# Two borders of a convolution kernel: six products for the statistics, other PSUM banks, and two relus in another place

## The chip, the cores and the metric

The kernel runs on one core of one Trainium2 chip. The metric is the device time of one execution in microseconds (us). The engines are named as the profile names them: PE is TensorE, DVE is VectorE, ACT is ScalarE, POOL is GpSimd, and SP is SyncE, which here only issues DMAs.

## The reference

Two bottleneck blocks run one after the other on an input of 64 images, 1024 channels and 14x14 pixels, all in f32. Each block is

```
out = relu(bn(conv1x1(x,   1024 -> 256)))
out = relu(bn(conv3x3(out,  256 -> 256)))
out =      bn(conv1x1(out,  256 -> 1024))
x   = relu(x + softplus(residual_scale) * out)
```

and bn takes its mean and variance over all images and pixels of the batch (12,544 values a channel). So a norm's scale and shift are known only after the whole batch has been through the convolution in front of it.

## The kernel before, in words

There are 128 partitions (P), so 1024 channels are 8 slots of 128 (CS) and 256 channels are 2 (MS). The batch is cut into 32 tiles of two images (T tiles of PX = 392 pixels). The 256-channel activations y of the whole batch stay in on-chip memory; x is streamed from memory, tile by tile, and block 0 leaves its output in memory as mid.

A block has these stages. The first 1x1 convolution (for block 0 at the start; for block 1 it is fused with the end of block 0), the 3x3 convolution (`conv2`, whose loads, columns and sums fill most of the profile), the Gram stage with the statistics of the third convolution, and the third convolution with the residual.

The statistics of the third convolution are not taken from its output. Its output is linear in y, so the mean of an output channel is its weights times the mean of y, and its variance is the weights on both sides of the 256x256 Gram matrix of y. `gram` builds the Gram matrix on PE: it transposes pieces of y and multiplies them with themselves into two PSUM banks, `upper` and `lower`, of which only some 64-wide blocks are computed, each off-diagonal block once. `conv3_stats` (from L1178 on) then does the following:

- `scaled` (L1185) moves the blocks from PSUM into two 128x258 tiles g0 and g1 (one for each half of the channels) with a DVE multiply by 1/n, or 2/n for a block that stands for itself and its mirror image. The blocks that are not there are zeros.
- ACT copies one column (L1193), DVE makes by_mean, the weights times the means, in two rows of 128x1024 (L1201, L1202).
- For each half h of the output channels, PE makes two 128x512 products t0 and t1, one for each half of the columns of g, each summed over g0 and g1: four matmuls a half, eight in all. DVE multiplies them by the weights (L1213) and adds the two (L1214).
- Sixteen matmuls with ones sum over the partitions: eight of by_mean into bank ax, eight of the products into bank ap. From the two, `affine` makes scale and shift of each output channel in a chain of short DVE operations (L1338 to L1357, L1498), with a square root on ACT between.

The order of each engine comes from a scheduler, but matmuls, most ACT operations and some DVE operations are kept in program order (`keep_in_program_order`). PE's matmuls all go through the helper at L171, ACT's through the one at L334, so these two lines stand for many operations and the tile names tell them apart.

[...] In block 0 they are named cy (two), ay (two), cx, cp, ap and ax; in block 1 cy, cx and cp (two each), ap and ax. Whoever asks for a tag whose banks are taken waits until the last reader is done. `psum.cycle` gives the tags where no tag is asked for.

The third convolution of the first tile of a block (o runs over the 8 slots of output channels, one `conv3` each) is plain. The result for o = 0 is made before the statistics, to fill PE; then o = 1, and in block 1 also o = 2 to 5, are made after them, before the affine. The list of these is `made`. `residual` (L1225 on) then takes for each o the made tile, or makes it, adds it to x on DVE (L1233: x = result*scale + x), applies the relu with the shift on ACT (L1234), and after the last o stores the tile (L1239, on POOL's queue when a whole tile is stored).

After it the other tiles of block 0 go through `fused`: a seven-product scheme (class `Seven`, two slots of output channels and two halves of the pixels at a time) for the third convolution (class `Conv3`, banks with prefix c) which is interleaved matmul by matmul with the same scheme for the first convolution of block 1 (class `Conv1`, prefix a). The third convolution has a lead of LAG = 14 steps, so PE does those alone first:

```
        for i in range(LAG):
            next(c)
```

The first steps of such a stream are p1 (bank cy), p2 (bank cx), p6 (again into cy), p5 (bank cp) and p7 (cy again). Between p1 and p6, and between p6 and p7, ACT has to copy the sum so far out of cy (tile cu12, L334), so each waits for ACT. POOL adds these copies to x (L488, L493), ACT applies the relu, and ACT's queue stores the tile. In block 1, `final` runs the same scheme for pairs of tiles and stores the output from SP's queue, which also loads x from mid.

Of the kernel before, what the change touches and what calls it, by code (L numbers as in the profile page):

```python
# [41 lines left out]
P = 128  # L42
# [46 lines left out]
def bottlenecks(ctx: ExitStack, tc: tile.TileContext, x, w1s, w2s, w3s, pars, out):  # L89
# [79 lines left out]
    def matmul(*args, **kw):  # L169

        tc.keep_in_program_order(nc.tensor.matmul(*args, **kw))  # L171
# [1006 lines left out]
    def conv3_stats(psum, one, grams, w3, mv, tags, spare):  # L1178
# [7 lines left out]

        scaled(g0[low], 0, upper[low], by[0][low])
        scaled(g0[high], Q + 1, upper[high], by[0][high])
        scaled(g1[low], 2 * Q + 1, lower[low, : 2 * Q + 1], by[1][low])
        n = Q + 1  # L1190
        for a, k in (1, 0), (3 * Q + 1, 1):
            scaled(g1[high], a, lower[high, k * n : k * n + n], by[1][high, k * n : k * n + n])
# [12 lines left out]
        for h in range(2):  # L1205
            cols = slice(h * half, (h + 1) * half)
            t0, t1 = (psum.tile(half * P, tag) for tag in tags[2 * h : 2 * h + 2])
            for i, g in enumerate((g0, g1)):
                for n, t in enumerate((t0, t1)):
                    matmul(t, g[:, 1 + n * P : 1 + n * P + P], w3[:, i, cols, :], start=i == 0, stop=i == 1)  # L1210
            qs = [q[:, s, h * half * P : (h + 1) * half * P] for s in range(MS)]
            for s, t in ((0, t0), (1, t1)):
                nc.vector.tensor_mul(qs[s], t, w3[:, s, cols, :].rearrange("p o c -> p (o c)"))  # L1213
            nc.vector.tensor_add(qs[0], qs[0], qs[1])  # L1214
# [10 lines left out]
    def residual(psum, xt, b, t, w3, aff, made=()):  # L1225
# [4 lines left out]
        for o in range(CS):  # L1230
# [3 lines left out]
            nc.scalar.activation(v, v, AF.Relu, bias=shift[:, o : o + 1])  # L1234

            step = CS if not tail else 1 if o + 2 >= CS else 2
            if (o + 1) % step == 0:
                queue = nc.gpsimd if step == CS else nc.scalar if o + 1 == CS else nc.sync
                queue.dma_start(  # L1239
                    out=to[:, (o + 1 - step) * PX : (o + 1) * PX],  # L1240
                    in_=xt[:, o + 1 - step : o + 1, :].rearrange("p s f -> p (s f)"),
                )

# [26 lines left out]
    def fused(psum, pool, xpool, xs, w1, w3, aff, par, stats, one_done):  # L1270
# [185 lines left out]
    for b in range(2):  # L1456
# [7 lines left out]
        with tc.tile_pool(name=f"last_{b}", bufs=1) as one, tc.tile_pool(  # L1464
# [6 lines left out]
            with ExitStack() as scope:  # L1471
# [22 lines left out]
                if b == 1:  # L1494
                    made += [conv3(psum, 0, o, w3, tag) for o, tag in zip(range(2, 6), ("cy", "cp") * 2)]
# [4 lines left out]
                residual(psum, xs[0], b, 0, w3, aff, made)  # L1500
                weights = made_a + made_c
                with tc.tile_pool(name=f"rest_{b}", bufs=1) as pool:
# [5 lines left out]
                    fused(psum, pool, xpool, xs, *weights, aff, par[b + 1], stats1, one_done)  # L1508
# [40 lines left out]
```

## Time and profile before

| | us |
|---|---|
| median of 3 runs (lowest to highest) | 1932.78 (1932.09 to 1934.12) |
| time of the profiled execution | 1934.62 |
| its span in the profile | 1932.8 |
| busy in the span: PE, DVE, ACT, POOL | 1907.8, 1545.2, 1080.9, 563.8 |
| statistics of block 0 (first product with g to last sum) | 653.21 to about 663.6 |
| statistics of block 1 | 1614.98 to about 1625.4 |

A line of the timeline has the start in us, the duration in us, the engine, the line of kernel.py, the operation, the tile that is written and those that are read, the shapes, and how many records are taken together; in brackets follow the idle time of the engine just before it and what ended that. An f32 matmul of this kernel leaves two records. Matmuls overlap in the pipeline, so the distance from one start to the next tells what one costs. A line of the waits says who waited for whom, for how many us in total, how often, and the longest.

### The profile page before, as it was taken

What the parts mean: (1) busy time and instruction counts of PE and PEld (TensorE: products, weight loads), DVE (VectorE), ACT (ScalarE), POOL (GpSimd) and SP (SyncE); (2) the same over time, 40 slices, a digit from 0 to 9 for tenths busy, and PEclk for the clock granted to TensorE, in tenths of its full rate; (3) what the DMA queues carried; (4) which work ended last, traced back from release to release, by engine and by line L of the source; (5) the groups of instructions that cost most, each with busy time, mean ns of one, the idle gap of its engine ahead of it and who ended that gap; (6) DMA issues with size and microseconds to landing.
All of it is one profiled execution on the core that took longest, in us unless ns stands there. A gap on an engine that the chain in (4) does not pass through costs nothing.

```text
span 1932.8 us, 28746 instructions
## 1 busy us (share of the span) xinstructions
PE 1907.8 (99%) x10246; PEld 1602.5 (83%) x10246; DVE 1545.2 (80%) x2481; ACT 1080.9 (56%) x2142; POOL 563.8 (29%) x680
## 2 busy tenths in 40 slices
PE   9999999999999999999999999999999999999999
PEld 5555557999997799999999999989999977555555
DVE  5778767999997767676776767689999986888886
ACT  2222214677777255555555555556777682666666
POOL 0111100211204133333433334302121041666664
PEclk9999999999999999999999999999999999999999
DMA  7777634787946534444444444258788466899998
GB/s 290 276 244 271 229 136 156 198 221 208 226 153 178 183 150 184 168 167 171 180 183 167 167 174 179 115 179 211 215 206 225 131 175 228 289 326 337 338 339 302
DMA packets 199071, 409.56 MB, mean 212 GB/s; under 512 B 37168, under 2 KB 175536, under 8 KB 182416
## 3 DMA queue, kind: packets, MB, share of 16 engines
q1 hardware_dynamic: 160128, 322.40, 48.4%
q0 software_dynamic: 33184, 34.25, 8.6%
q10 hardware_dynamic: 5616, 51.06, 6.3%
q8 instruction: 81, 1.33, 0.3%
q14 instruction: 62, 0.51, 0.1%
HBM read 263.75 MB, written 115.34 MB: 196 GB/s over the span
## 4 chain that ended last, share of the span: by engine, by line
PE 93%; DVE 3%; DMA 1%; ACT 1%; issue 1%; SPq 0%; POOL 0%; DVEq 0%; ACTq 0%; POOLq 0%
PE cy L171 17%; PE ay L171 17%; PE columns L171 13%; PE cp L171 12%; PE ap L171 10%; PE m L171 7%; PE l L171 6%; PE cx L171 5%; PE ax L171 4%; PE ps L171 1%; ACT y L334 0%; DMA home<-y 0%; DMA x<-mid 0%; SPq L1065 0%; DMA ws<-y 0%
## 5 line engine op out<-in xcount | busy, mean ns | idle before, releaser
L334 ACT ACTIVATE cu<-cy,scale 128x196 f32<-128x196 f32 (+1 forms) x552 | 256.8, 474 | 276.9 <-PE cy L171 271.7
L171 PE MATMUL columns<-v,ub 128*128 128x224 f32 (+1 forms) x1536 | 300.7, 337 | 0.0
L334 ACT ACTIVATE x<-x,shift 128x392 f32<-128x392 f32 x428 | 241.0, 613 | 59.6 <-POOL x L493 53.1
L171 PEld LDWEIGHTS columns<-v,ub 128*128 128x128 f32 x1536 | 269.2, 188 | 2.8
L467 DVE SCALAR_TENSOR_TENSOR x<-cp,scale,x 128x196 f32<-128x196 f32 (+1 forms) x368 | 178.0, 484 | 97.8 <-PE cp L171 96.5
L171 PE MATMUL cy<-ct,ws 128*128 128x196 f32 (+1 forms) x736 | 221.9, 383 | 1.8 <-ACT cu L334 1.7
L488 POOL TENSOR_TENSOR x<-x,cu 128x196 f32<-128x196 f32 (+1 forms) x184 | 159.7, 868 | 172.9 <-ACT cu L334 165.0
L171 PE MATMUL ay<-at,ws 128*128 128x196 f32 (+1 forms) x752 | 209.1, 381 | 0.0
L493 POOL TENSOR_TENSOR x<-x,cu 128x392 f32<-128x392 f32 x124 | 125.8, 1014 | 191.5 <-DVE x L467 191.5
L171 PEld LDWEIGHTS ay<-at,ws 128*128 128x128 f32 x752 | 136.5, 190 | 33.4
L171 PEld LDWEIGHTS cy<-ct,ws 128*128 128x128 f32 x736 | 133.4, 190 | 37.0 <-ACT cu L334 5.3
L171 PE MATMUL l<-diffs,ub 128*128 128x224 f32 (+1 forms) x768 | 149.1, 337 | 2.6 <-PE columns L171 2.6
L514 POOL TENSOR_TENSOR x<-x,cu 128x392 f32<-128x392 f32 x120 | 122.0, 1017 | 86.2 <-DVE x L467 71.8
L171 PE MATMUL m<-sums,ua 128*128 128x224 f32 (+1 forms) x752 | 145.9, 337 | 1.1 <-DVE sums L625 1.1
L334 ACT ACTIVATE au<-ay 128x196 f32<-128x196 f32 (+1 forms) x141 | 53.8, 381 | 156.9 <-PE ay L171 152.1
L171 PEld LDWEIGHTS l<-diffs,ub 128*128 128x128 f32 x768 | 134.3, 189 | 4.4 <-PE columns L171 3.9
L467 DVE SCALAR_TENSOR_TENSOR x<-cx,scale,x 128x196 f32<-128x196 f32 (+1 forms) x184 | 89.0, 484 | 57.0 <-PE cx L171 56.8
L171 PEld LDWEIGHTS m<-sums,ua 128*128 128x128 f32 x752 | 131.3, 189 | 2.9 <-DVE sums L625 2.5
L171 PE MATMUL cy<-y,w 128*128 128x196 f32 (+1 forms) x408 | 125.3, 393 | 0.0
L171 PE MATMUL cx<-y,w 128*128 128x196 f32 (+1 forms) x400 | 122.7, 391 | 0.0
L171 PE MATMUL cp<-y,ws 128*128 128x196 f32 (+1 forms) x368 | 113.6, 390 | 0.2 <-DVE x L467 0.2
L761 ACT ACTIVATE columns<-m 128x448 f32<-128x448 f32 (+1 forms) x160 | 78.5, 490 | 59.4 <-PE m L171 56.8
(219 smaller groups left out, 3973.1 us busy)
## 6 DMA issues: line engine op xcount, KB each, us to landing
x<-in_x SPq DMA_DIRECT2D x62, 1568.0 KB, 6.6
ub<-u SPq DMA_DIRECT2D x94, 768.0 KB, 5.3
x<-mid SPq DMA_DIRECT2D x32, 1568.0 KB, 7.8
mid<-x ACTq DMA_DIRECT2D x31, 1568.0 KB, 5.1
out<-x SPq DMA_DIRECT2D x123, 392.0 KB, 5.4
ua<-u SPq DMA_DIRECT2D x94, 256.0 KB, 3.0
u<-y POOLq DMA_DIRECT2D x48, 256.0 KB, 5.6
home<-y SPq DMA_DIRECT2D x72, 96.0 KB, 3.6
```

The lines of the kernel that those rows point to most:

```text
L171: tc.keep_in_program_order(nc.tensor.matmul(*args, **kw))
L334: tc.keep_in_program_order(nc.scalar.activation(*args, **kw))
L467: nc.vector.scalar_tensor_tensor(v, bank, self.scale[:, o : o + 1], v, ALU.mult, ALU.add)
L488: nc.gpsimd.tensor_add(self.part(1, 1), self.part(1, 1), u3)
L493: nc.gpsimd.tensor_add(v, v, self.u12)
L514: nc.gpsimd.tensor_add(v, v, self.u12[:, i * self.n : (i + 1) * self.n])
L761: nc.scalar.activation(v, m, AF.Copy)
```

## The change

There are three edits, of which the first concerns both blocks and the others only block 0.

1. In `conv3_stats` the block of the Gram matrix that stood left of the diagonal (rows of g1, columns of g0's half) is transposed on PE into bank ax and copied by DVE into the empty place of g0 that mirrors it. With it the left half of g1 holds nothing that a product needs, so t0 takes one matmul (g0) and t1 two (g0 and g1): six in all instead of eight. The block to be transposed is scaled first in the source.
2. In block 0, `made` holds five tiles before the affine instead of two, with tags ay, ay, cy, cx, cy, and the tags of the last three are given by a new `psum.cycle`.
3. In block 0, the relus of the last two output slots of the first tile and its store are not issued in `residual`. They are collected in a list, and `fused` issues them after the third step of the stream's lead. The relus now go through the helper at L334.

```diff
@@ conv3_stats
+        n = Q + 1
+        scaled(g1[high], 1, lower[high, :n], by[1][high, :n])
+        turned = psum.tile(P, "ax")
+        tc.keep_in_program_order(nc.tensor.transpose(turned, g1[:, 1 : P + 1], ident))
         scaled(g0[low], 0, upper[low], by[0][low])
         scaled(g0[high], Q + 1, upper[high], by[0][high])
+        nc.vector.tensor_copy(g0[low, 3 * Q + 1 : M + 1], turned[low, Q:])
         scaled(g1[low], 2 * Q + 1, lower[low, : 2 * Q + 1], by[1][low])
-        n = Q + 1
-        for a, k in (1, 0), (3 * Q + 1, 1):
-            scaled(g1[high], a, lower[high, k * n : k * n + n], by[1][high, k * n : k * n + n])
+        scaled(g1[high], 3 * Q + 1, lower[high, n : 2 * n], by[1][high, n : 2 * n])
...
-            for i, g in enumerate((g0, g1)):
-                for n, t in enumerate((t0, t1)):
-                    matmul(t, g[:, 1 + n * P : 1 + n * P + P], w3[:, i, cols, :], start=i == 0, stop=i == 1)
+            left, right = slice(1, P + 1), slice(P + 1, M + 1)
+            matmul(t0, g0[:, left], w3[:, 0, cols, :], start=True, stop=True)
+            matmul(t1, g0[:, right], w3[:, 0, cols, :], start=True, stop=False)
+            matmul(t1, g1[:, right], w3[:, 1, cols, :], start=False, stop=True)
@@ residual
-            nc.scalar.activation(v, v, AF.Relu, bias=shift[:, o : o + 1])
+            relu = partial(act, v, v, AF.Relu, bias=shift[:, o : o + 1])
+            if later is not None and o + 2 >= CS:
+                later.append(relu)
+            else:
+                relu()
...
-                queue.dma_start(
+                store = partial(
+                    queue.dma_start,
...
+                if later is not None:
+                    later.append(store)
+                else:
+                    store()
@@ fused
         for i in range(LAG):
             next(c)
+            if i == 2:
+                for run in begun:
+                    run()
@@ bottlenecks
-                if b == 1:
-                    made += [conv3(psum, 0, o, w3, tag) for o, tag in zip(range(2, 6), ("cy", "cp") * 2)]
+                tags = ("cy", "cp") * 2 if b else ("cy", "cx", "cy")
+                made += [conv3(psum, 0, 2 + i, w3, tag) for i, tag in enumerate(tags)]
+                if b == 0:
+                    psum.cycle = itertools.cycle(["ay", "ay", "cy"])
...
-                residual(psum, xs[0], b, 0, w3, aff, made)
+                later = None if b else []
+                residual(psum, xs[0], b, 0, w3, aff, made, later)
...
-                    fused(psum, pool, xpool, xs, *weights, aff, par[b + 1], stats1, one_done)
+                    fused(psum, pool, xpool, xs, *weights, aff, par[b + 1], stats1, one_done, later)
```

More of the change, by code (lines that the diff above doesn't have):

```diff
@@ L1223, in conv3_stats, with residual @@
         nc.vector.tensor_sub(mv[:, :, 1], mv[:, :, 1], sq)
-    def residual(psum, xt, b, t, w3, aff, made=()):
+    def residual(psum, xt, b, t, w3, aff, made=(), later=None):
         scale, shift = aff
@@ L1268, in final, with fused @@
         residual(psum, xs[T - 1], 1, T - 1, a, aff)
-    def fused(psum, pool, xpool, xs, w1, w3, aff, par, stats, one_done):
+    def fused(psum, pool, xpool, xs, w1, w3, aff, par, stats, one_done, begun):
         def last_convs():
```

## The prediction

> **What bounds the kernel now.** I read the page's busy line first, then the chain of work that ended last, then PE's own waits between 653 and 690 us, and then the timeline of PE and DVE at the two borders (about 651 to 690 us for block 0, 1613 to 1640 us for block 1).
>
> ```profile
> PE 1907.8 (99%) x10246; PEld 1602.5 (83%) x10246; DVE 1545.2 (80%) x2481; ACT 1080.9 (56%) x2142; POOL 563.8 (29%) x680
> PE 93%; DVE 3%; DMA 1%; ACT 1%; issue 1%; SPq 0%; POOL 0%; DVEq 0%; ACTq 0%; POOLq 0%
> ```
>
> PE is busy 99% of the span and makes 93% of the chain. So a microsecond counts if it is PE work, or PE's waiting, and only there. The waits of PE in the first border:
>
> ```profile
> PE cy L171 <- ACT cu L334: 1.6, 3, 1.0
> PE ay L171 <- DVE x L1233: 1.2, 1, 1.2
> ```
>
> The timeline of PE shows where they stand:
>
> ```profile
> 653.21 1.02 PE L171 MATMUL cy<-w,g 128*128 128x512 f32 x2
> 654.07 1.02 PE L171 MATMUL cp<-w,g 128*128 128x512 f32 x2
> ...
> 660.08 1.89 PE L171 MATMUL ax<-ones,home 128*128 128x64 f32 x16
> 661.81 1.95 PE L171 MATMUL ap<-ones,home 128*128 128x64 f32 x16
> 663.60 1.53 PE L171 MATMUL ay<-y,w 128*128 128x392 f32 x4
> 664.97 1.48 PE L171 MATMUL cy<-y,w 128*128 128x392 f32 x4
> 667.60 1.55 PE L171 MATMUL ay<-y,w 128*128 128x392 f32 x4 [1.15 <-DVE x L1233]
> ...
> 676.11 0.60 PE L171 MATMUL cy<-ct,ws 128*128 128x196 f32 x2 [1.02 <-ACT cu L334]
> 676.54 0.49 PE L171 MATMUL cp<-ct,ws 128*128 128x196 f32 x2
> 677.22 0.60 PE L171 MATMUL cy<-ct,ws 128*128 128x196 f32 x2 [0.18 <-ACT cu L334]
> ...
> 681.93 0.60 PE L171 MATMUL cy<-ct,w 128*128 128x196 f32 x2 [0.41 <-ACT cu L334]
> ```
>
> The eight products with g run from 653.21 to 660.08: 6.87 us, 0.86 us each (each leaves two records), with no gap. Four waits follow: 1.15, 1.02, 0.18 and 0.41 us. Block 1 has the same eight products (1614.98 to 1621.85) and one wait of 0.53 us at 1636.65. DVE at the start of the statistics:
>
> ```profile
> 651.75 0.74 DVE L1185 TENSOR_TENSOR g<-cp,by 64x193 f32<-64x193 f32 x2 [2.31 <-PE cp L171]
> 652.52 0.69 DVE L1185 TENSOR_TENSOR g<-ap,by 64x129 f32<-64x129 f32 x3
> 653.24 0.75 DVE L1201 TENSOR_SCALAR home<-w,g 128x1024 f32<-128x1024 f32 x1
> ```
>
> [...] This trace has 128x128 f32 transposes of 271 to 329 ns (L1086), four of them 0.59 us apart from the next work, so about 0.15 us each in a row. [...] the granted clock reads 1.00 in all stretches around the borders, so gaps cost only themselves. [...] L488 took 1.00 us at 678.42 beside such operations and 0.60 elsewhere.
>
> **The change, part by part.** Set side by side, the two programs have the same order on every engine outside the two borders, DMAs on SP and POOL included.
>
> *Six products and a transpose (both blocks).* Two products go: -2 x 0.86 = -1.72 us of PE. The transpose comes: +0.15 to 0.25 us of PE behind conv3's first tile. It waits for the first 65-wide scaled piece of g1, which the new DVE order puts second, ready near 652.35; PE comes to it at 653.15, so no wait. The first product (left half of g0) waits only for scaled pieces. The second (right half) waits for the copy of the transposed block. In DVE's queue that copy stands behind the first by_mean row (0.75 us, 653.24 to 653.99), so it ends near 654.2 (0.1 to 0.2 us, bounded by the 65-wide pieces, which come to about 0.2). With its weight load, 0.19 us (the LDWEIGHTS rows), the second product starts near 654.44, where 654.07 is today: 0.37 us late. Net 1.72 - 0.37 = 1.35 us per block. If the copy were earlier than I think, 1.55; if 0.3 us later, 1.05. Queued behind the copy is the second by_mean row (1.28 us), which becomes 0.2 us later and ends at 655.5; sums of it are wanted at 658.7. The multiplies of the products' results (0.69 us each) keep up: the last product ends at 658.7, multiply and add end near 660.35, the first eight sums at 660.45, and of the second eight only the fifth needs that add. So the statistics, affine and all that hangs on them come 1.35 us earlier.
>
> *Five tiles ahead in block 0, other banks.* Today only two tiles stand before affine; the third gets a bank at once, the fourth waits for the first residual to release one (1.15 us, with the restart 1.31 us against the even 1.32 us pitch). With ay, ay, cy, cx, cy the three tiles after the sums' first one take banks that the statistics have left (the last is read at about 660), so PE runs on. The sixth tile waits for the first residual: affine's chain, 663.79 to 666.83 today, ends near 665.5, residual 0 near 666.1; the sixth tile is due at 667.6. Slack 1.5 us. Gain 1.31 us. By the first product of the fused part PE is 1.35 + 1.31 = 2.66 us ahead, at 671.6 for 674.26.
>
> *Last two relus and the store later.* The chain today: residual 7 on DVE, relu 7 on ACT (to 675.65), then cu, then PE's third product at 676.11. With both relus behind that cu, it goes when its product ends: 671.6 + 0.53 = 672.1, + 0.42, + 0.06: third product at 672.6, 3.5 us earlier. But the relus now stand ahead of the second cu. Relu 6 and 7 take 1.15 us in a row, until 673.6; the second cu could have gone at 673.2. So 0.4 us of the gain goes back: the fifth product at 673.6 + 0.42 + 0.06 = 674.05, 3.17 us earlier than 677.22. Next late is the chain cu, L488, L493, two relus, cu, product (today 677.86 to 681.93). DVE now puts the two column sums (0.97 us each, two SBUF inputs) before it; the second ends near 675.9, and L488, ready at 675.1, waits for it. L493 ends near 677.45, and 1.53 us later, as today, PE gets its product at 678.98: 2.95 us earlier. Bounds: L488 not held, 3.4; both POOL adds at 1 us behind the sums, 2.5. The store on POOL is issued after relu 7, as today (676.03), about 2 us earlier, and the adds behind it wait for cu longer than that. Without that cover its 0.59 us would be added.
>
> Sum: block 0: 2.95 us (1.35 + 1.31 + 0.29 of ACT); block 1: 1.35; total 4.3 us. Nothing between takes it back: PE shows 10.00 of 10 us busy in each stretch that I read from 800 to 1100 us, while DVE, the next, is at 70%, and the order there is unchanged. The profiled execution took 1934.62 us with a span of 1932.8; the runs shown have a median of 1932.78, 1.84 us below it. So 4.3 off the span gives 1928.5, and off the median 1928.48. I forecast 1928.5.
>
> The last stage is where block 1's part could be lost:
>
> ```profile
> 1640.00:1860.00 220.00, 220.00 (x657) 122.21 (x656) 182.44 (x279) 148.94 (x282) 143.90 (x141) 1.00 0.91 321
> 1860.00:1870.00 10.00, 9.77 (x30) 5.20 (x29) 8.46 (x14) 6.43 (x14) 6.90 (x7) 1.00 0.99 372
> ```
>
> Its columns are PE, PEld, DVE, ACT, POOL, clock, DMA share and GB/s. PE is full, but the transfers hold 0.91. One load is already late (0.23 us of PE at 1864.7).
>
> **The rivals.** *Main case*, both borders keep their gain: 1927.7 to 1929.2; chance 0.62.
>
> *The last stage belongs to the transfers*: block 1's 1.35 us is waited off at loads: 1928.5 + 1.35 = 1929.8. For: 0.91 to 0.99 shares, the late load. Against: one wait in 290 us, and DMA's share is only 0.36 and 0.45 just before and after the border (1613 to 1624, 1624 to 1640), so its work can move up too. Chance 0.12.
>
> *ACT and POOL return more*: the late relus and the copy each cost their upper bound: block 0 2.5 - 0.3, block 1 1.05: 3.25 us, 1929.5. This is "the wait moved, not removed". For: three of the four old waits are on ACT's cu and the relus stay in that queue. Chance 0.12.
>
> *More is won*: L488 unheld and the copy early: 3.6 + 1.55 = 5.15, 1927.6 or a little below. Chance 0.08.
>
> *Slower*: one mechanism, the loads from mid in the last stage. SP issues stores and loads in one queue; if the moved start changes which store a load waits behind, loads that now land just in time land late. It has taken the whole gain when the last stage waits 4.3 us for loads (today 0.23), and is slower by 0.2% at 8.2 us; with 13 pairs of loads from 1660 on, 0.63 us a pair, which gives 1936.7. Against: the shares leave 9% of 220 us, 20 us, free, and the queue order is the same. Chance 0.06.
>
> **How the numbers follow.** About 0.2%, 3.87 us, is what a measurement here can tell from no change: below 1928.91 is faster, above 1936.65 slower. The main case ends mostly below that line (0.62, of which 0.12 falls above it), and more-won adds 0.08: faster 0.58. The two small-gain cases and the main case's upper end: same 0.37. Of the last case 0.05 reaches slower and 0.01 counts as same. The range 1927.2 to 1930.8 holds main, more-won and the two small-gain cases with a run's own spread (1932.09 to 1934.12 around the old median), and leaves some 0.15 out; the likeliest one's own is 1927.7 to 1929.2.
>
> **What would show it.** PE: six products with g of 0.86 us; the second starts 1.0 to 1.3 us after the first, not 0.86. No wait on L1233 before the sixth tile. Start of the fused part's third product about 3.5 us, and of its product at 681.93 about 3 us earlier; a gap of about 0.6 us before the fifth. DVE: the copy right after the first by_mean row. At 1614 the same 1.35 us. I am wrong if PE waits over 0.5 us for the copy, if a wait for cu over 1 us remains, if the lead of block 0 is not found again at 1275 us, or if the last stage waits over 1 us for x from mid.

## The result, and the profile after

| | before | after |
|---|---|---|
| median of 20 runs each on one chip, us (lowest to highest) | 1932.95 (1930.72 to 1937.29) | 1930.24 (1926.61 to 1932.67) |
| ratio after/before, 95% interval | | 0.9982 (0.9976 to 0.9989) |
| profiled execution, us, and its span | 1934.62, 1932.8 | 1932.67, 1930.9 |
| mean granted TensorE clock of the profiled execution | 0.999 | 0.998 |

The changed kernel is 2.7 us, 0.18%, faster. The forecast was 1928.5 (4.3 us faster) with a range of 1927.2 to 1930.8. The time lies in the range, but outside the 1927.7 to 1929.2 of the likeliest case: the gain is under the 0.2% (3.87 us) that the forecast took as the line between "faster" and "same". So the question is what became of 1.6 us. The two profiled spans differ by only 1.9 us, so even more seems to be missing there.

The busy line and the chain of the page of the changed kernel look as before; PE is busy for 0.6 us less, in six fewer records:

```profile
PE 1907.2 (99%) x10240; PEld 1602.1 (83%) x10240; DVE 1545.3 (80%) x2483; ACT 1080.9 (56%) x2142; POOL 563.6 (29%) x680
PE 92%; DVE 4%; ACT 1%; issue 1%; DMA 1%; SPq 0%; POOL 0%; DVEq 0%; ACTq 0%; POOLq 0%
```

The busy time can't carry the argument. Four products of 0.86 us are gone, 3.4 us of work, and two transposes came, but PE's busy time falls by 0.6 us only. About 1.7 us of the difference is other work of this execution that ran at a lower clock (0.83 from 610 to 620 us), as shown below; the rest I did not trace. The border of a block (from its first made tile, through the statistics and the residual, to the first products of the seven-product stream) has to be read for itself. The timeline of PE in the changed kernel at the border of block 0:

```profile
654.57 1.58 PE L171 MATMUL ay<-y,w 128*128 128x392 f32 x4
655.99 0.27 PE L1190 MATMUL ax<-ident,g 128*128 128x128 f32 x1
656.10 1.02 PE L171 MATMUL cy<-w,g 128*128 128x512 f32 x2
657.08 1.98 PE L171 MATMUL cp<-w,g 128*128 128x512 f32 x4
658.90 1.02 PE L171 MATMUL cy<-w,g 128*128 128x512 f32 x2
659.75 1.88 PE L171 MATMUL cx<-w,g 128*128 128x512 f32 x4
661.47 1.89 PE L171 MATMUL ax<-ones,home 128*128 128x64 f32 x16
...
664.99 1.54 PE L171 MATMUL ay<-y,w 128*128 128x392 f32 x4
666.36 1.48 PE L171 MATMUL cy<-y,w 128*128 128x392 f32 x4
667.68 1.48 PE L171 MATMUL cx<-y,w 128*128 128x392 f32 x4
668.99 1.48 PE L171 MATMUL cy<-y,w 128*128 128x392 f32 x4
670.31 2.80 PE L171 MATMUL ay<-y,w 128*128 128x392 f32 x8
...
675.35 0.60 PE L171 MATMUL cy<-ct,ws 128*128 128x196 f32 x2 [0.26 <-ACT cu L334]
675.79 0.49 PE L171 MATMUL cp<-ct,ws 128*128 128x196 f32 x2
676.68 0.60 PE L171 MATMUL cy<-ct,ws 128*128 128x196 f32 x2 [0.40 <-ACT cu L334]
...
681.60 0.60 PE L171 MATMUL cy<-ct,w 128*128 128x196 f32 x2 [0.53 <-ACT cu L334]
```

Six products with g stand between the transpose and the ones: one, two, one, two. The transpose takes its place for 0.11 us (655.99 to 656.10). The tiles that follow run on at a pitch of 1.3 us; the wait on L1233 (1.15 us before) is gone. Of the three waits for cu, 1.02, 0.18 and 0.41 us before, stand 0.26, 0.40 and 0.53.

Now each mark is measured from the start of the first made tile (651.79 before, 654.57 after), so that what ran ahead of the border drops out:

| gain at the mark, us | forecast | measured |
|---|---|---|
| block 0, first product with ones | 1.35 | 1.39 (8.29 to 6.90) |
| first product of the fused part | 2.66 | 2.78 |
| third product of the fused part | 3.5 | 3.54 |
| its fifth product | 3.17 | 3.32 |
| product at 681.93 before, 681.60 after | 2.95 | 3.11 (30.14 to 27.03) |
| block 1, first product with ones | 1.35 | 1.39 (8.29 to 6.90) |

From that product at block 0 to the first made tile of block 1 it is 931.63 us before and 931.70 after. From block 1's third product to the end of the span it is 296.15 and 295.9. The last stage was where the prediction feared for block 1's part. Its two stretches in the changed kernel (columns: stretch, length, PE, PEld, DVE, ACT and POOL busy, granted clock, DMA share, GB/s) show PE full in both, and the late load is not there:

```profile
1640.00:1860.00 220.00, 220.00 (x657) 122.01 (x656) 183.03 (x280) 149.60 (x282) 143.88 (x142) 1.00 0.91 322
1860.00:1870.00 10.00, 10.00 (x32) 5.54 (x31) 8.40 (x14) 6.36 (x12) 6.73 (x8) 1.00 1.01 371
```

So the places that the change touches gain 3.11 + 1.39 = 4.5 us, what lies between keeps it, and the last stage is 0.25 us shorter in this pair of profiles (the experiments show that this part does not come from the change). But the border itself began 2.78 us later in the profile of the changed kernel, behind a part where the two programs are the same, and 4.5 + 0.25 - 0.07 - 2.78 = 1.9 us is the difference of the spans.

Where those 2.78 us come from, the profile shows too. About 1.1 us are there when PE gets its first Gram product after its longest wait, the one for zt in the Gram stage (612.15 us before, 613.25 after). zt is the transposed piece of y that the product multiplies; DVE makes it from a piece that a DMA brings. Part of the 1.1 us is a wait of 0.6 us for the first loads of x, which the profile of before does not list. The rest of the 2.78, 1.68 us, follows at once. The wait in the kernel before, then DVE's transpose behind the late transfer in the changed kernel:

```profile
612.15 0.55 PE L171 MATMUL cp<-zt 128*64 128x193 f32 x4 [2.91 <-DVE zt L1102]
```

```profile
612.48 1.30 DVE L1102 STREAM_TRANSPOSE zt<-ws 128x512 f32<-128x512 f32 x2 [4.47 <-DMA home<-y]
```

The same stretch of 10 us in the kernel before, then in the changed kernel, with the columns as above:

```profile
610.00:620.00 10.00, 7.85 (x114) 7.41 (x116) 8.61 (x13) 5.67 (x6) 2.73 (x5) 1.00 0.54 134
```

```profile
610.00:620.00 10.00, 7.22 (x82) 6.28 (x80) 7.52 (x12) 6.00 (x6) 2.72 (x5) 0.83 0.51 135
```

The granted clock of the stretch is 0.83 in the changed kernel and 1.00 in the kernel before. PE's timeline in the changed kernel:

```profile
610.08 0.40 PE L171 MATMUL ap<-zt 128*64 128x129 f32 x4
613.25 0.81 PE L171 MATMUL cp<-zt 128*64 128x193 f32 x4 [2.78 <-DVE zt L1102]
...
614.27 0.87 PE L171 MATMUL cp<-zt 128*64 128x193 f32 x4
...
615.35 0.87 PE L171 MATMUL cp<-zt 128*64 128x193 f32 x4
...
616.42 0.70 PE L171 MATMUL cp<-zt 128*64 128x193 f32 x4
...
617.17 0.50 PE L171 MATMUL cp<-zt 128*64 128x193 f32 x4
```

From 613.25 to about 616.7 us the Gram products run at half speed (1.07 us from one cp group to the next, 0.55 us later), and then at full speed again; such a stretch at half speed is called a dip from here on. Half speed over 3.4 us costs 1.7 us (measured from the end of the wait to the first made tile: 41.32 us, against 39.64 in the kernel before). The kernel before had such a wait at the same place, 2.91 us, and no dip behind it, but one behind the same wait in block 1 (0.83 from 1570 to 1580 us), and so had the changed kernel. That this belongs to the execution and not to the change had to be shown.

### The profile page after: what moved, and what is told of

Same layout as the page of the kernel before. It is cut to its first block, busy times and chain, and to the rows that moved or that the text cites. A ratio compares the mean times of both kernels' runs of the same rounds, so it can differ in the third digit from the quotient of the medians.

```text
span 1930.9 us, 28737 instructions
## 1 busy us (share of the span) xinstructions
PE 1907.2 (99%) x10240; PEld 1602.1 (83%) x10240; DVE 1545.3 (80%) x2483; ACT 1080.9 (56%) x2142; POOL 563.6 (29%) x680
## 4 chain that ended last, share of the span: by engine, by line
PE 92%; DVE 4%; ACT 1%; issue 1%; DMA 1%; SPq 0%; POOL 0%; DVEq 0%; ACTq 0%; POOLq 0%
PE cy L171 17%; PE ay L171 17%; PE columns L171 13%; PE cp L171 12%; PE ap L171 10%; PE m L171 7%; PE l L171 6%; PE cx L171 5%; PE ax L171 4%; PE ps L171 1%; DMA home<-y 0%; ACT y L334 0%; DVE v L631 0%; DMA x<-in_x 0%; DVE sums L625 0%
## 5 line engine op out<-in xcount | busy, mean ns | idle before, releaser
L334 ACT ACTIVATE cu<-cy,scale 128x196 f32<-128x196 f32 (+1 forms) x552 | 256.7, 474 | 277.2 <-PE cy L171 272.1
L334 ACT ACTIVATE x<-x,shift 128x392 f32<-128x392 f32 x452 | 255.0, 613 | 73.1 <-POOL x L493 54.0
L467 DVE SCALAR_TENSOR_TENSOR x<-cp,scale,x 128x196 f32<-128x196 f32 (+1 forms) x368 | 178.0, 484 | 97.2 <-PE cp L171 96.0
L488 POOL TENSOR_TENSOR x<-x,cu 128x196 f32<-128x196 f32 (+1 forms) x184 | 159.6, 867 | 171.7 <-ACT cu L334 163.8
L334 ACT ACTIVATE au<-ay 128x196 f32<-128x196 f32 (+1 forms) x141 | 53.8, 382 | 158.0 <-PE ay L171 155.2
L467 DVE SCALAR_TENSOR_TENSOR x<-cx,scale,x 128x196 f32<-128x196 f32 (+1 forms) x184 | 89.0, 484 | 56.7 <-PE cx L171 56.5
```

The lines of the kernel that those rows point to most:

```text
L334: tc.keep_in_program_order(nc.scalar.activation(*args, **kw))
L467: nc.vector.scalar_tensor_tensor(v, bank, self.scale[:, o : o + 1], v, ALU.mult, ALU.add)
L488: nc.gpsimd.tensor_add(self.part(1, 1), self.part(1, 1), u3)
```

## The experiments

Theory A: the change gains what the borders show, 4.4 to 4.5 us, and all of it reaches the end; the rest of the difference is scatter of single executions. Theory B: a part of the gain is given back elsewhere, by a lower clock or in the last stage. A second pair of theories, set up later, is on the source of the scatter: theory C, it comes from the wait for zt and the dip behind it; theory D, the clock falls by itself, whatever PE does there.

The local intervals of the profiled executions, in us:

| | wait for zt, block 0 | first made tile starts | to first ones | to the product at 681.93 | between the borders | block 1: to first ones | to third product | from there to the end |
|---|---|---|---|---|---|---|---|---|
| before | 2.91 | 651.79 | 8.29 | 30.14 | 931.63 | 8.29 | 23.09 | 296.15 |
| c_null | 2.75, dip | 653.81 | 8.29 | 30.14 | 928.88 | 8.29 | 23.09 | 296.18 |
| after | 2.78, dip | 654.57 | 6.90 | 27.03 | 931.70 | 6.90 | 21.70 | 295.9 |
| c_after | 3.33, dip | 653.89 | 6.91 | 27.03 | 930.85 | 6.92 | 21.72 | 295.91 |
| c_six | 2.77, dip | 653.25 | 6.91 | 28.71 | 929.67 | 6.91 | 21.71 | 295.86 |
| c_rest | 3.64, dip | 654.25 | 8.29 | 28.42 | 929.69 | 8.29 | 23.09 | 296.35 |
| d_nolate | 2.71 | 652.30 | 6.91 | 27.47 | 930.23 | 6.90 | 21.70 | 295.9 |
| d_split | 2.56, dip | 653.86 | 6.90 | 26.40 | 931.55 | 6.91 | 21.71 | 295.88 |
| d_actcopy | 3.85, dip | 655.82 | 6.68 | 26.17 | 929.84 | 6.68 | 21.48 | 296.29 |

### The kernel before, and the changed kernel, once more

Without an edit. These two say how far two executions of one program lie apart, in the whole and in the borders.

> The kernel before, unchanged, as a control. Both theories expect no difference to the kernel before (ratio 1.000). What its runs scatter, with the granted clock of each, is what the other comparisons have to be read against: if runs of one program differ by 3 us, and the slower ones have the lower clock, then single profiles and medians of a few runs can't settle 2 us.

> The changed kernel again. Theory A (the local gains all reach the end; the median of 2.7 us came from scatter of the first loads and of the clock): about 4.5 us less than before, ratio 0.9977, and the same mix of granted clocks as before. Theory B (part is given back[...]): about 2.7 us less, ratio 0.9986, and lower granted clocks than the kernel before on the same chip. In the trace both expect 6.9 us from the first tile's start to the first sum at both borders.

Measured: the kernel before against itself 1934.51 (1931.62 to 1937.64), ratio 1.0004 (0.9995 to 1.0013); the changed kernel 1931.08 (1927.05 to 1934.68), ratio 0.9983 (0.9974 to 0.9992). By its ratio and its clock c_after looks more like theory B: the ratio is nearer to B's 0.9986 than to A's 0.9977, and its runs have a mean clock of 0.9988, where those of the kernel before on that chip have 0.9993. But the unedited c_null, timed beside it, has 0.9989. The scatter alone makes such a difference, and these two runs do not decide between A and B.

The table's rows agree within 0.02 us in every interval at the borders, for both programs (e_after and the filled kernels below within 0.03), but the start of the border moves by 2.0 us between the two profiles of the kernel before, and the stretch between the borders by 2.75. So the borders repeat to a few hundredths and the parts around them only to some microseconds. The second execution of the unchanged program has the dip and the late start: the change does not bring them.

### The six products alone, and the rest alone

c_six is the kernel before with only the new `conv3_stats`; c_rest is the changed kernel with the old one.

```diff
@@ c_rest
-        scaled(g1[high], 1, lower[high, :n], by[1][high, :n])
-        turned = psum.tile(P, "ax")
-        tc.keep_in_program_order(nc.tensor.transpose(turned, g1[:, 1 : P + 1], ident))
...
-            matmul(t0, g0[:, left], w3[:, 0, cols, :], start=True, stop=True)
-            matmul(t1, g0[:, right], w3[:, 0, cols, :], start=True, stop=False)
-            matmul(t1, g1[:, right], w3[:, 1, cols, :], start=False, stop=True)
+            for i, g in enumerate((g0, g1)):
+                for n, t in enumerate((t0, t1)):
+                    matmul(t, g[:, 1 + n * P : 1 + n * P + P], w3[:, i, cols, :], start=i == 0, stop=i == 1)
```

> The six products with the transposed block alone, in both blocks; banks, made tiles and relus as before. Theory A: from the first tile's start to the first product with ones 6.90 us instead of 8.29 at both borders, nothing else moves, so 2 x 1.39 = 2.8 us less (ratio 0.9986). Theory B: the same in the trace, but about 1.7 us in the time. A rival for block 1, that the transfers of the last stage take its share back: only 1.4 us less, and waits of PE or DVE for x from mid after 1640 us.

> The other banks and five made tiles with the late relus, with the eight products of before. Theory A: block 0's border 1.3 us shorter at the fused part's first product, and 1.7 us shorter at the product that stood at 681.93 (3.11 less 1.39), so 1.7 us less in the time (ratio 0.9991). If the parts are not additive, for instance because the lead of the six products is needed to make the sixth tile come without a wait, a wait for L1237's residual stays and the gain is under 1 us.

Measured: c_six 1932.12 (1927.58 to 1935.09), ratio 0.9989 (0.9981 to 0.9996); c_rest 1933.24 (1929.81 to 1936.07), ratio 0.9996 (0.9990 to 1.0002). Theory A's 0.9986 and 0.9991 lie inside both intervals. In the profiles c_six gains 1.43 us by the product at 681.93 and 1.38 in block 1, c_rest 1.72 us in block 0 and nothing in block 1. 1.43 + 1.72 = 3.15, against 3.11 for both edits together: the parts add up. The timeline of PE in c_six shows that the six products alone move the four waits and leave them in size:

```profile
667.59 1.58 PE L171 MATMUL ay<-y,w 128*128 128x392 f32 x4 [1.06 <-DVE x L1237]
...
676.12 0.60 PE L171 MATMUL cy<-ct,ws 128*128 128x196 f32 x2 [1.02 <-ACT cu L334]
...
677.24 0.60 PE L171 MATMUL cy<-ct,ws 128*128 128x196 f32 x2 [0.18 <-ACT cu L334]
...
681.96 0.60 PE L171 MATMUL cy<-ct,w 128*128 128x196 f32 x2 [0.42 <-ACT cu L334]
```

The banks and the relus are what takes the wait for the first residual and most of the 1.02 us; in c_rest the waits are 0.27, 0.40 and 0.54 us, those of the changed kernel within 0.01. The medians alone could not have parted c_rest from the kernel before.

### The relus in their old place

d_nolate keeps the six products and the banks, and issues the two relus and the store in `residual`.

```diff
-                for run in begun:
+                for run in begun or ():
...
-                later = None if b else []
+                later = None
```

> The changed kernel without the late relus (they and the store are issued in the residual as before). If the late relus are what shortens the wait of the third product of the fused part: that wait grows from 0.26 to about 1.0 us and the one before the fifth falls from 0.40 to 0.18; at the product that stood at 681.60 the kernel is about 0.3 us later than the changed one. In the time under 0.5 us, no clear difference. If they do more than that (because L488 and the relus behind it also move), 1 us later or more.

Measured: 1929.96 (1926.0 to 1933.87), ratio 0.9977 (0.9968 to 0.9986), not told apart from the changed kernel by its time. The profile is clearer: 27.47 us to the product at 681.93 instead of 27.03, so the third edit is worth 0.44 us (0.52 by the waits alone). PE's timeline in d_nolate:

```profile
673.95 0.60 PE L171 MATMUL cy<-ct,ws 128*128 128x196 f32 x2 [1.12 <-ACT cu L334]
...
675.06 0.60 PE L171 MATMUL cy<-ct,ws 128*128 128x196 f32 x2 [0.18 <-ACT cu L334]
...
679.77 0.60 PE L171 MATMUL cy<-ct,w 128*128 128x196 f32 x2 [0.41 <-ACT cu L334]
```

The first wait for cu is 1.12 us with the relus ahead of it and 0.26 with them behind, so 0.86 us is taken from it; 0.22 and 0.12 us go back at the next two. The last of these is not ACT's. Its chain goes over POOL's L488, whose group in the changed kernel's timeline is

```profile
677.89 1.20 POOL L488 TENSOR_TENSOR x<-x,cu 128x196 f32<-128x196 f32 x1 [0.69 <-ACT cu L334]
```

and DVE's queue beside it

```profile
676.66 0.96 DVE L400 TENSOR_TENSOR at<-x 128x784 f32<-128x784 f32 x1
677.66 0.97 DVE L401 TENSOR_TENSOR at<-at,x 128x784 f32<-128x784 f32 x1
```

L488 starts within L401's time and ends 0.46 us after it; alone it takes 0.60 us. In the kernel before L488 met one of these sums too, L419, and took 1.00 us:

```profile
678.42 1.00 POOL L488 TENSOR_TENSOR x<-x,cu 128x196 f32<-128x196 f32 x1 [1.80 <-ACT cu L334]
```

```profile
678.01 0.96 DVE L419 TENSOR_TENSOR at<-x,at 128x784 f32<-128x784 f32 x1
```

It ends 0.45 us after L419. This holds beyond the border: from 670 to 900 us of the two profiles, 24 of L488's operations of this shape start beside such a sum of DVE (0.60 us becomes 1.00 to 1.35), and every one ends 0.45 to 0.47 us after the sum does, whenever it started; those that start beside none take 0.59 to 0.61 us.

### One relu behind each of two copies

d_split issues the first late relu after the third step of the lead, as the change does, and the second with the store after the fourth.

```diff
             if i == 2:
-                for run in begun:
+                begun[0]()
+            elif i == 3:
+                for run in begun[1:]:
                     run()
```

> The changed kernel with the two late relus in two places: relu 6 after the third step of the lead, relu 7 and the store after the fourth. If it is the two relus in a row in front of the second cu that make the 0.40 us wait before the fifth product: that wait falls to about 0.1 to 0.2 us, and 0.2 us are won there. At the next product with a wait (0.53 us) the chain runs through POOL, so if the column sum L401, which now stands behind four residuals, no longer holds L488, that one falls by 0.3 us more. In the time 0.2 to 0.5 us less than the changed kernel.

Measured: 1928.31 (1926.18 to 1931.21), ratio 0.9971 (0.9960 to 0.9982). To the product at 681.93 it is 26.40 us, 0.63 less than in the changed kernel, where 0.2 and 0.3 had been expected for the two causes. The waits in that border of d_split and its L488:

```profile
PE cy L171 <- ACT cu L334: 0.8, 3, 0.4
```

```profile
677.16 0.60 POOL L488 TENSOR_TENSOR x<-x,cu 128x196 f32<-128x196 f32 x1
```

With a relu less ahead of it, the second cu goes when its product ends (wait 0.18 instead of 0.40), and L488 takes 0.60 us instead of 1.20. For the latter the edit is only a remote cause. The scheduler put L401 behind four of DVE's L467 (678.84 instead of the place before them), so that L488 met only the last 0.06 us of L400. The two causes were moved by one edit; the run does not part them beyond these two durations.

### The copy of the transposed block on ACT

d_actcopy is d_split with the copy out of bank ax on ACT, where no by_mean row is ahead of it.

```diff
-        nc.vector.tensor_copy(g0[low, 3 * Q + 1 : M + 1], turned[low, Q:])
+        act(g0[low, 3 * Q + 1 : M + 1], turned[low, Q:], AF.Copy)
```

> As the one with the relus in two places, and the transposed block copied by ACT instead of DVE. If the second product with g waits 0.12 us because the copy stands behind the by_mean row on DVE: that wait goes at both borders (the second product starts 0.86 us after the first, not 0.98), 6.78 us instead of 6.90 from the first tile's start to the first sum, so 0.24 us less in all. If ACT's copy is no earlier than DVE's, nothing changes.

Measured: 1927.82 (1924.63 to 1931.42), ratio 0.9966 (0.9955 to 0.9978). Each border is shorter by 0.22 us (6.90 to 6.68), where 0.12 had been expected. The timeline of PE in d_actcopy and the copy:

```profile
657.24 0.27 PE L1190 MATMUL ax<-ident,g 128*128 128x128 f32 x1
657.35 1.02 PE L171 MATMUL cy<-w,g 128*128 128x512 f32 x2
658.21 1.88 PE L171 MATMUL cp<-w,g 128*128 128x512 f32 x4
659.92 1.02 PE L171 MATMUL cy<-w,g 128*128 128x512 f32 x2
```

```profile
657.54 0.22 ACT L334 ACTIVATE g<-ax 64x64 f32<-64x64 f32 x1 [0.59 <-PE ax L1190]
```

The second product now follows the first by 0.86 us, with no wait; in the changed kernel it was 0.98. And the pair that begins with it takes 1.71 us until the next product, where the changed kernel takes 1.82 (657.08 to 658.90). So a wait of 0.12 us for the copy cost 0.22: the pair behind it was 0.10 us slower. In DVE's queue of the changed kernel the place of the copy is what the forecast had said, behind the first by_mean row:

```profile
656.02 0.75 DVE L1204 TENSOR_SCALAR home<-w,g 128x1024 f32<-128x1024 f32 x1
656.80 0.22 DVE L1193 COPY g<-ax 64x64 f32<-64x64 f32 x1
656.94 1.27 DVE L1205 SCALAR_TENSOR_TENSOR home<-w,g,home 128x1024 f32<-128x1024 f32 x1
```

### The same relus moved in block 1

d_both is d_actcopy with the late relus and store in block 1 as well, where one wait for cu of 0.53 us was left.

```diff
-        for _ in stream(pairs(), (T // 2 - 1) * CS // 2):
-            pass
+        for i, _ in enumerate(stream(pairs(), (T // 2 - 1) * CS // 2)):
+            if i == 2:
+                begun[0]()
+            elif i == 3:
+                for run in begun[1:]:
+                    run()
...
-                later = None if b else []
+                later = []
```

> As the last one, and the late relus, split in the same way, in block 1's first tile as well. If the 0.53 us wait of the third product there (1636.65 us before) is relu 7 in front of cu, as the chain of before has it: it goes, 0.5 us less at block 1's border. If the transfers of the last stage bound the end, the lead of 0.5 us is not found at the end. In the time about 5.4 us less than before (ratio 0.9972), 0.9 us less than the changed kernel.

Measured: 1928.09 (1925.33 to 1930.97), ratio 0.9967 (0.9956 to 0.9978). PE's waits from 1610 us on, in d_actcopy and in d_both:

```profile
PE cy L171 <- ACT cu L334: 0.5, 1, 0.5
```

```profile
PE cp L171 <- DVE x L467: 0.2, 1, 0.2
```

The wait for cu is gone and the next mark comes 0.42 us earlier, but a wait of 0.2 us for x appears in the last stage, which the kernel before has too. The time is not told apart from d_actcopy's. Both are ahead of the changed kernel; by how much is told with the clock below, since they were timed on another chip than the result above. In d_actcopy's profile 0.4 us of its lead over d_split is gone at the end again (296.29 us from the third product on, 295.88 in d_split), without a wait of PE that names a cause; d_both does not settle that (296.44 us by the same mark, after its own 0.42 us of lead).

### The wait for zt filled with idle products

The wait of PE for zt ends, by way of DVE's transpose, with a transfer that lands late in the middle of the Gram stage, in both blocks. e_fill is the changed kernel with three products of 128x448, which nothing reads, right ahead of the product that waits; e_fillboth is d_both, and e_fillbefore the kernel before, with the same edit. e_after is the changed kernel once more.

```diff
+            if k == 14:
+                busy(psum, "ax", 3)
             if before is not None:
                 for c in range(CH):
```

> The changed kernel once more, as the base for e_fill on the same chip. Both theories: ratio to the kernel before 0.9975 to 0.9990, mean granted clocks of its runs spread over 0.998 to 1.000, times spread over some 6 us. In its profile PE waits 2 to 3.5 us for zt near 610 us, and where the clock is below 0.99 in a stretch of 10 us, that stretch is the one after this wait, the one after the same wait near 1570 us, or the end.

> The changed kernel with three idle products (128x448, about 2.2 us together, nothing reads them) put into PE's queue right ahead of the Gram product that waits for zt, in both blocks. Theory C, the scatter of the medians comes from this wait, after which the clock falls to half for some 3.4 us in a part of the executions (1.7 us each time): the wait shrinks to under 1 us, no stretch at 610 to 620 or 1570 to 1580 us is below 0.99, nearly all runs have a mean clock of 0.999 or 1.000, and the median is 1 to 2 us below e_after with a narrower spread (some 4 us). Theory D, the clock falls by itself whatever PE does there: clocks and spread as in e_after, median the same or up to 0.6 us higher (the products are longer than the wait of block 1 in some executions).

> d_both with the same three idle products in both blocks. Theory C: as e_fill against e_after, so about 1.5 us further under the kernel before than d_both (5.5 us at equal clock), 6.5 to 8 us, ratio 0.9958 to 0.9967, clocks 0.999 to 1.000. Theory D: as d_both, ratio 0.9967 to 0.9972, clocks 0.998 to 1.000.

> The kernel before with the same three idle products ahead of the Gram product that waits for zt. With the scatter gone its runs should lie within 1 us of each other for the most part, as those of e_fill did (1929.44 to 1930.08 for 16 of 18). If the change is worth what the borders show (theory A), the median is e_fill's 1929.78 plus 4.5 us, 1934.0 to 1934.6; if a part is given back elsewhere and the 2.7 us of the first comparison are its true size (theory B), it is 1932.3 to 1932.8.

| | median, us (lowest to highest, runs) | ratio to before on the same chip, 95% |
|---|---|---|
| e_after | 1929.52 (1926.65 to 1931.97, 12) | 0.9978 (0.9969 to 0.9986) |
| e_fill | 1929.78 (1929.44 to 1931.68, 18) | 0.9978 (0.9971 to 0.9985) |
| e_fillboth | 1927.82 (1927.36 to 1928.89, 8) | 0.9972 (0.9962 to 0.9982) |
| e_fillbefore | 1934.09 (1933.0 to 1935.22, 13) | 1.0001 (0.9992 to 1.0009) |

The timeline of PE in e_fill at the place, and its stretch of 10 us:

```profile
609.66 3.18 PE L171 MATMUL ax<-ident 128*128 128x448 f32 x6
612.99 0.55 PE L171 MATMUL cp<-zt 128*64 128x193 f32 x4
```

```profile
610.00:620.00 10.00, 9.73 (x108) 7.19 (x108) 7.78 (x12) 5.35 (x6) 2.73 (x5) 1.00 0.47 123
```

Nothing is left of the wait in PE's list, the clock is 1.00, and 16 of the 18 runs lie between 1929.44 and 1930.08, where e_after's spread over 5.3 us. The other two filled kernels spread over 1.5 us (e_fillboth) and 2.2 us (e_fillbefore, for which about 1 us had been expected), where the unfilled ones spread over 5 to 8. So C holds on the scatter: the wait of varying length, with the dip behind it, makes most of it. C was wrong on the median, which did not fall; e_fill's lies where D had it, and e_fillboth gained 6.0 us on the kernel before, where C had 6.5 to 8. The three products take 3.1 us (a record of 3.18), not 2.2, as much as the wait itself and more than it in block 1 (1.6 to 2.8 us), so what the dips cost goes into the products.

With most of the scatter gone, the change can be measured: e_fillbefore's median less e_fill's is 4.31 us (3.9 to 4.8, the 95% interval when the runs are drawn again at random), the difference of the means 4.2 ± 0.4. The expectation for a full gain had been 1934.0 to 1934.6, for a part given back 1932.3 to 1932.8: it is 1934.09. The two were timed on two chips; the kernel before took 1933.81 us on e_fill's and 1933.47 on e_fillbefore's, so the chips do not make the difference. Theory A stands.

### What the clock says over all runs

Each timed run has its mean granted clock. I fitted the times of 300 runs with one term per kernel and one common term for the clock (140 runs of the kernel before, 46 of the changed kernel, the rest those of the experiments; one unit is 0.001 of the clock, to which it is rounded). 0.001 of the clock costs 2.06 us (95% 1.87 to 2.25), about 0.1% of the span. At equal clock, against the kernel before (with a term for each chip as well, the first row is -4.54 ± 0.51, and no chip differs by more than 0.5 us):

| | us at equal clock, 95% | local gain at both borders, us |
|---|---|---|
| after | -4.44 ± 0.39 | -4.50 |
| c_six | -2.49 ± 0.59 | -2.81 |
| c_rest | -1.57 ± 0.53 | -1.72 |
| d_nolate | -4.21 ± 0.64 | -4.06 |
| d_split | -5.21 ± 0.89 | -5.12 |
| d_actcopy | -6.09 ± 0.89 | -5.58 |
| d_both | -5.61 ± 0.83 | -6.0 |

The last column adds, for each kernel, the gain to the product at 681.93 and the gain to block 1's first ones (for d_both its 0.42 us besides). The times follow the local gains, each within its interval. By this, d_actcopy and d_both are 1.2 to 1.6 us ahead of the changed kernel, with intervals of 0.9; with the wait filled, e_fillboth is 2.0 us ahead of e_fill on the same chip, and its slowest run is faster than e_fill's fastest.

The mean clock of the runs is 0.99926 for the kernel before, 0.99902 for the changed kernel, and 0.9999 for the three filled ones, with either order of the border. The 0.0002 between the first two may be chance: c_null, the same program as the kernel before, has 0.9989. Where the wait is filled, the clock is 0.9999 in both orders and the gain is there: fewer gaps at the border went with no lower clock here. What the runs leave open is whether the change makes the dip a little more frequent; the clocks put that at 0.5 ± 0.5 us.

In the eleven profiles without the filler, the dip stands behind 10 of the 22 long waits for zt (the longest of each block): behind none of the eight shorter than 2.3 us, and behind ten of the fourteen from 2.32 to 3.85 us. It also accounts for the largest steps in the table: from the end of the wait to the first made tile it is 39.63 to 39.64 us in the profiles without it and 41.30 to 41.32 with it (42.08 in d_actcopy, whose stretch reads 0.66 because the clock was at half for 6.8 us, from within the wait on), and the three longest ways between the borders (931.55 to 931.70) are those with a dip in block 1. That the wait and not something else of the transfer behind it triggers the dip is shown by the filled kernels only in this: with PE busy over the same time, no dip came in three profiles.

## Why the prediction was right or wrong

**Six products and a transpose: right, 1.39 for 1.35 us per block.** The copy stood where forecast. The second product came 0.98 us after the first (forecast 1.0 to 1.3), and 0.23 us late against its old place where 0.37 had been forecast. The copy was not early: it ended 2.45 us after the first tile's start, where the working has 2.41. The difference is the weight load behind it, which the working counted whole before the product:

```profile
657.07 0.30 PEld L171 LDWEIGHTS cp<-w,g 128*128 128x128 f32 x2 [0.78 <-DVE g L1193]
```

The product's record begins 0.01 us after that of its load (657.08). In return the pair behind the wait is 0.10 us slower, which the working did not have; whether that is the load's time coming back is not shown. The two errors, 0.14 and 0.10 us, nearly cancel, so the nearness of 1.39 to 1.35 is in part luck. Of the two the copy cost the more: 0.22 us, which d_actcopy wins back; the transpose has a record of 0.27 us, but its price in the stream is the distance of 0.11 us to the next start.

**Five tiles ahead: right.** No wait is left on the residual (forecast gain 1.31 us; measured 2.78 - 1.39 = 1.39 us by the first fused product). c_six, which keeps the two tiles, has 1.06 us of that wait.

**Relus and store later: right in the mechanism and within 0.16 us.** Forecast: third product 3.5 us earlier, then 0.3 given back at the fifth by the relus ahead of the second cu, and 0.2 more by L488 behind the column sums. Measured: 3.54, 0.22 and 0.21. (The prediction's text says that 0.4 us goes back, its own times give 0.34; the gap before the fifth product, forecast near 0.6 us, was 0.40.) Of L488 the forecast said that it waits for the sums, which was the author's estimate; in the profile it starts beside L401 and is stretched to 1.20 us. In all 24 cases L488 ends 0.45 to 0.47 us after the sum beside it, less than the 0.60 us that it takes alone, so it does not wait for the sum with the whole of its work; and d_split, where only the last 0.06 us of a sum is beside it, has 0.60 us. What holds it up is not shown.

**"Nothing between takes it back": right.** 931.63 and 931.70 us between the borders (each with a dip in block 1's Gram stage), and PE is full in the last stage. With it falls the rival that the transfers own the last stage, which would have taken 1.35 us: over all fourteen profiles the way from block 1's third product to the end is 295.86 to 296.44 us. It does not go by the order of the border either. e_fillbefore, in the old order, has 295.86, and e_fill, in the new one, 296.24; the 0.25 us that the first pair of profiles gained there is such a difference. The slower case falls in the same way: PE waits for x in the last stage for 0.4 us at most (e_fillboth), and in eight of the fourteen profiles not at all.

**The rivals of size.** "ACT and POOL return more" (3.25 us) and "more is won" (5.15 us) had opposite values for L488 and the copy. The measured borders, 4.5 us, lie between; d_split and d_actcopy show that 0.63 us in block 0 and 0.22 us per border could indeed be won there.

**Where it was off: the step from the sum to the median.** The prediction set 4.3 us off the median of three runs and gave 0.58 to a median more than 3.87 us lower. (That 4.3 off the profiled span gives the same 1928.5 is no second support: the time of that execution is 1.8 us above its span.) The sum was good to 0.2 us: at equal clock the gain is 4.44 ± 0.39, with the wait filled 4.31 (3.9 to 4.8), where 4.3 had been forecast. But a run of the kernel before lies anywhere from 1930.2 to 1938.1 over the chips used here, and the first comparison's ratio leaves 2.1 to 4.6 us open. With a forecast of 4.3 and a line at 3.87, the line lay inside that scatter, and more of the main case's 0.62 belonged above it than the 0.12 it was given.

None of the prediction's four signs of being wrong appeared: the wait for the copy was 0.12 us, the longest for cu 0.53, the lead was kept, and the last stage waited under 1 us.

What stood behind the scatter was in the profile of before: PE's wait for zt, 5.7 us in two times, was its longest, with a dip behind the second, and the prediction did not count it because the change leaves it alone. Its sentence that gaps cost only themselves, with the granted clock at 1.00 around the borders, was argued for the borders and holds there for the clock: no wait in them, 1.15 us at most, was followed by a dip. It was no ground for taking the rest of the span as fixed. A dip at half speed lasted 3.4 us in nine of ten times, and whether one came varied from execution to execution. The length of the wait alone does not tell: one of 2.32 us (d_split, block 1) was followed by a dip, and one of 3.55 us (e_after) by none.

## What to carry to other kernels

Compare two traces by intervals between marks of the same program, counted from a mark just ahead of the edit: here they repeated to 0.03 us, while spans of one program differed by microseconds, and so parts of 0.2 us, a hundredth of a percent, could be told. Where the runs scatter, look for the longest wait of the engine that bounds the kernel, even if the edit is far from it, and fill it in both kernels for the comparison: here that took the spread from 5.3 us to 0.6 for 16 of 18 runs and brought out the gain. Where a copy stands between two products of that engine, ask what is ahead of it in its own queue and whether another engine is idle there; and spread work that is moved behind a wait over several such places, since here all in one place made the next wait longer (0.40 us, and 0.18 with the relus over two places).

## What was unexpected of the hardware

- After a wait of 2.32 to 3.85 us for zt PE ran at half speed in ten of fourteen cases: nine times for 3.4 us, at a cost of about 1.7 us, and once, after the longest wait, for 6.8 us with a part of it inside the wait, at a cost of 2.4 (d_actcopy). It never did after the eight shorter waits (0.85 to 2.17 us).
- POOL's add of 128x196 f32 took 0.60 us alone; begun beside a two-input sum of DVE it ended 0.45 to 0.47 us after the sum did, in 24 of 24 cases.
- A 128x128 f32 transpose took PE 0.11 us from its start to the next product's, in a record of 0.27 us.
- A wait of 0.12 us for a product's operand cost 0.22 us: the pair that begins with that product took 1.82 us instead of 1.71.
- The copy of 64x64 f32 from PSUM took 0.22 us on DVE and on ACT alike.
- Three idle products of 128x448 f32 took 3.1 us (3.10 to 3.11 to the next product's start in five of six places, 3.33 once), where 2.2 had been estimated from the columns (a product of 128x512 takes 0.86 in the borders).
